# A graph layer on one Trainium2 core: three rearrangements in the second layer's small matmuls

## The chip, the cores and the metric

The kernel runs on one core of a Trainium2 chip. The metric is the device time of one execution in microseconds (us). Before the change it was 2445.93 us, the median of three runs (2436.05 to 2448.57).

## What is computed

64 graphs of 256 nodes with 256 features each go through two layers, each followed by a residual and a layer norm. Everything is fp32. The reference, cut to what matters here:

```python
# layer 0
norm_adj = d_inv_sqrt[:, :, None] * adj * d_inv_sqrt[:, None, :]
x = layernorm(x + ((norm_adj + alpha * eye) @ x) @ W.T + b)

# layer 1
xc = transpose(x)                                   # features x nodes
h = relu(bn1(conv1d(xc, conv1_w)))                  # conv1: one tap, 256 -> 256
h = bn2(conv1d(h, conv2_w))                         # conv2: 17 taps along the nodes
x_conv = transpose(relu(h + xc))
s = x @ w_se.T + b_se                               # 3 numbers per node
sq = sum(s * s, axis=-1)
dist = sq[:, :, None] + sq[:, None, :] - 2.0 * einsum('bnd,bmd->bnm', s, s)
A = exp(-dist) * adj
x_nmp = A @ relu(x @ w_msg.T + b_msg)
# a GRU cell with input [x_conv, x_nmp] and hidden state x follows, then
x = layernorm(x + gru(x_in, x))
```

## The kernel before

The 17-tap convolution is done with short Fourier transforms: the 256 nodes of a graph are cut into 16 tiles of 16 nodes, each tile is transformed with its surroundings (32 values per tile and feature), and for each frequency one product with the transformed weights is taken for 8 graphs at once. So the kernel works in rounds of 8 graphs: the graphs' first part (`layer0`, `layer1`), then the products per frequency and the transforms back on VectorE, then the GRU (`gru`), whose matmuls are mixed among those of the next round. The functions are generators; at each `yield` another one may put its instructions in, and a scheduler then fixes the order on each engine.

`layer1` of one graph, whole but for its last lines:

```python
    def layer1(g, V):
        x1, adjT = X1.pop(g), ADJT.pop(g)
        xn = work.tile([P, 2 * DCH, N], F32, name="xn")
        x1T = xn[:, :DCH]
        p = bank("p_x1T").rearrange("p (k n) -> p k n", k=DCH)
        for k in range(DCH):
            for c in range(NCH):
                nc.tensor.transpose(p[:, k, c * P : (c + 1) * P], x1[:, c, k * P : (k + 1) * P], ident)
        nc.scalar.copy(x1T, p)
        yield
        p = bank("p_s")
        for k in range(DCH):
            nc.tensor.matmul(p[:96, :N], wse[:, k, :], x1T[:, k], start=k == 0, stop=k == DCH - 1)
        nc.vector.tensor_scalar(dl[0:32, :], p[0:32, :N], bse[0:32], None, op0=ALU.add)
        nc.vector.tensor_scalar(dr[0:32, :], p[0:32, :N], bse[0:32], 2.0, op0=ALU.add, op1=ALU.mult)
        nc.scalar.activation(dr[32:64, :], p[32:64, :N], AF.Square, bias=bse[32:64])
        nc.scalar.activation(dl[64:96, :], p[64:96, :N], AF.Square, bias=bse[64:96])

        h = work.tile([P, NCH, D], F32, name="h", bufs=1)
        p = bank("p_conv1").rearrange("p (c o) -> p c o", c=NCH)
        # p[:, c, :] = x1T[:, k, chunk c].T @ wc1[:, k, :], 4 matmuls of 256 columns
        nc.vector.tensor_tensor(h, p, bn1_bias.unsqueeze(1).to_broadcast([P, NCH, D]), op=ALU.add)
        nc.scalar.activation(h, h, AF.Relu)
        yield
        # p_msg: 4 matmuls with wmsg, then the bias (VectorE) and the relu (ScalarE) into msg
        yield
        aT = work.tile([P, NCH, 2, P], F32, name="aT", bufs=1)
        p = bank("p_dist").rearrange("p (c n) -> p c n", c=NCH)
        for c in range(NCH):
            nc.tensor.matmul(p[:, c, :], dl[:, c * P : (c + 1) * P], dr, start=True, stop=True)
        nc.scalar.activation(aT.rearrange("p c n q -> p c (n q)"), p, AF.Exp)
        nc.vector.tensor_mul(aT, aT, adjT[:, :, 0:3:2, :])
        yield
        mid = GT // 2
        for k in range(DCH):
            p = bank("p_dft")
            for c, t0, t1 in ((0, 0, mid + 1), (1, mid + 1, GT), (1, mid - 1, mid + 1)):
                first = t0 + 1 - c * mid
                nc.tensor.matmul(
                    p[:, t0 * FL : t1 * FL], h[:, c, k * P : (k + 1) * P],
                    fwd[:, first : first + t1 - t0, :].rearrange("p t f -> p (t f)"),
                    start=t0 == 0, stop=t1 == mid + 1 and c == 1,
                )
            nc.scalar.copy(
                V[:, :, k, g % Q * GT : (g % Q + 1) * GT], p.rearrange("p (t f) -> p f t", f=FL)
            )
        yield
        # p_nmp: 4 matmuls of msg with aT; copied into xn and stored for the GRU
        ...
```

N = D = 256, P = 128, NCH = DCH = 2 chunks, GT = 16 tiles, FL = 32. `bank` takes one of three PSUM banks in turn. `dl` and `dr` hold three groups of 32 rows: s against 2s, -1 against s squared, s squared against -1, so that one matmul over 96 rows gives minus the distances. `layer0` of a later graph (its matmuls are p_adjT, p_hT, p_out) is mixed in between these parts, and so are the GRU's p_rz and p_n.

## Time and profile before

| | |
|---|---|
| span in the profile | 2444.4 us |
| TensorE (PE) busy | 2327.9 us, 9440 records |
| VectorE (DVE) busy | 1406.5 us, 3231 instructions |
| ScalarE (ACT) busy | 748.6 us |
| GpSimd (POOL) busy | 530.2 us |
| DMA | 289.73 MB, mean 119 GB/s |
| granted TensorE clock | 0.979 of full speed |

The groups of instructions that the change touches, as the profile gives them (records, mean duration of one):

| line, engine | what | records | mean ns |
|---|---|---|---|
| L364 PE | p_s, 256 columns | 256 | 397 |
| L374 PE | p_conv, 256 columns | 512 | 382 |
| L396 PE | p_dist, 96 rows, 256 columns | 256 | 379 |
| L407 PE | p_dft, 288 / 224 / 64 columns | 256 each | 423 / 352 / 247 |
| L358 PE | p_x1T, transposes of 128 columns | 256 | 278 |
| L365, L366 DVE | s and 2s out of PSUM, 32x256 | 64 each | 469, 463 |
| L377 DVE | bias of conv1, 128x512 | 64 | 684 |
| L367, L368 ACT | squares out of PSUM, 32x256 | 64 each | 467, 465 |
| L397 ACT | exp out of PSUM, 128x512 | 64 | 595 |

In the profile the rows of an engine are groups of equal instructions with their source line, output and inputs. PE is TensorE's matmuls, PEld its weight loads. A matmul's recorded duration contains the time in the pipeline, and records overlap: what a matmul takes from the engine is seen in the distance between the starts of neighbours. "A waited for B" in the list of waits means that A's engine sat idle until B ended. The windows view gives, for a stretch of the span, the busy time and the number of instructions of PE, PEld, DVE, ACT and POOL, then the clock, the busy share of the DMA engines and their GB/s.

### The profile page before, as it was taken

How to read it: one execution, taken by the hardware profiler on the slowest of the kernel's cores; microseconds unless marked ns; L12 is line 12 of the kernel's file. 1: busy time of each engine (PE TensorE's matmuls, PEld its weight loads, DVE VectorE, ACT ScalarE, POOL GpSimd, SP SyncE). 2: the span in 40 equal slices, each digit the busy share in tenths (PEclk: the TensorE clock that was granted, in tenths of full speed). 3: DMA queues.
4: the chain of work that ended last, by engine and by line, in shares of the span. 5: the costliest groups of instructions: out<-in, count | busy, mean ns of one | idle time of the engine just before them, and what ended most of it. 6: DMA issues, size and time to landing. Idle time of an engine off the chain costs nothing.

```text
span 2444.4 us, 27289 instructions
## 1 busy us (share of the span) xinstructions
PE 2327.9 (95%) x9440; PEld 1714.9 (70%) x9440; DVE 1406.5 (58%) x3231; ACT 748.6 (31%) x1417; POOL 530.2 (22%) x581
## 2 busy tenths in 40 slices
PE   5999799999999999999999999999999999999997
PEld 4887577766777677776877667776677767776654
DVE  4344754576546755468445674457654674446744
ACT  2563153204441144311532124420444114431111
POOL 3221122112221122221221222211222112211122
PEclk8999999999999999999999999999999999999999
DMA  6557522462225522273223722246312552126221
GB/s 152 163 170 254 148 83 77 143 172 95 65 82 178 145 91 85 88 196 111 90 78 126 206 74 91 72 149 172 95 65 82 182 141 91 65 76 185 79 74 47
DMA packets 225890, 289.73 MB, mean 119 GB/s; under 512 B 19081, under 2 KB 202633, under 8 KB 224250
## 3 DMA queue, kind: packets, MB, share of 16 engines
q1 hardware_dynamic: 188986, 207.19, 27.8%
q0 software_dynamic: 33360, 79.88, 11.6%
q8 instruction: 75, 1.23, 0.2%
q10 hardware_dynamic: 3408, 0.93, 0.2%
q14 instruction: 61, 0.50, 0.1%
HBM read 208.46 MB, written 79.47 MB: 118 GB/s over the span
## 4 chain that ended last, share of the span: by engine, by line
PE 47%; issue 32%; POOL 8%; DVE 7%; DMA 3%; ACT 2%; POOLq 0%; ACTq 0%; SPq 0%; DVEq 0%
PE p_rz L633 8%; PE p_n L638 5%; PE p_nmp L420 5%; PE p_dft L407 4%; PE p_k L444 4%; PE p_msg L385 3%; PE p_conv L374 3%; PE p_out L339 3%; PE p_hT L329 3%; PE p_u L252 2%; POOL ln_rs L269 2%; POOL total L660 2%; POOL x_g L661 2%; PE p_s L364 2%; PE p_dist L396 2%
## 5 line engine op out<-in xcount | busy, mean ns | idle before, releaser
L633 PE MATMUL p_rz<-whh,xn_g 128*128 128x512 f32 x512 | 244.9, 594 | 0.0
L633 PE MATMUL p_rz<-wih,xcT 128*128 128x512 f32 x512 | 241.2, 593 | 0.0
L633 PE MATMUL p_rz<-wih,xn_g 128*128 128x512 f32 x512 | 240.6, 592 | 0.0
L642 DVE TENSOR_TENSOR trz<-p_rz,brz_t 128x512 f32<-128x512 f32 x128 | 87.7, 685 | 242.8 <-PE p_rz L633 242.8
L660 POOL TENSOR_TENSOR total<-x_g,nn 128x512 f32<-128x512 f32 x64 | 81.5, 1273 | 657.2 <-ACT nn L652 657.0
L444 PE MATMUL p_k<-u,V 128*128 128x256 f32 x960 | 220.0, 381 | 4.0 <-DMA u<-ud 3.6
L269 POOL TENSOR_TENSOR ln_rs<-ln_rs,neg_half 128x2 f32<-128x2 f32 x128 | 99.8, 780 | 549.6 <-DVE ln_rs L268 534.5
L643 ACT ACTIVATE trz<-trz 128x512 f32<-128x512 f32 x128 | 80.7, 630 | 422.8 <-DVE trz L642 379.4
L444 PEld LDWEIGHTS p_k<-u,V 128*128 128x128 f32 x960 | 181.1, 190 | 33.8 <-DMA u<-ud 4.5
L633 PEld LDWEIGHTS p_rz<-wih,xn_g 128*128 128x128 f32 x512 | 97.3, 190 | 119.3 <-issue 119.0
L633 PEld LDWEIGHTS p_rz<-wih,xcT 128*128 128x128 f32 x512 | 96.2, 190 | 114.8 <-issue 114.7
L638 PE MATMUL p_n<-whh,xn_g 128*128 128x256 f32 x512 | 139.9, 396 | 20.4 <-DVE trz L642 20.4
L645 DVE TENSOR_TENSOR gn<-p_n,bn_t 128x512 f32<-128x512 f32 x128 | 88.2, 689 | 119.3 <-PE p_n L638 118.7
L329 PE MATMUL p_hT<-adjT,x 128*128 128x256 f32 x512 | 127.6, 397 | 25.6 <-DVE ln_rs L268 11.0
L420 PE MATMUL p_nmp<-aT,msg 128*128 128x256 f32 x512 | 132.2, 404 | 17.4 <-DVE aT L398 17.4
L407 PEld LDWEIGHTS p_dft<-fwd,h 128*128 128x128 f32 x768 | 135.1, 190 | 18.0 <-ACT xcT L598 1.0
L407 PE MATMUL p_dft<-fwd,h 128*128 128x288 f32 (+2 forms) x768 | 146.9, 341 | 0.4 <-DVE x L343 0.4
L638 PEld LDWEIGHTS p_n<-whh,xn_g 128*128 128x128 f32 x512 | 98.7, 198 | 62.6 <-issue 27.5
L638 PE MATMUL p_n<-wih,xn_g 128*128 128x256 f32 x512 | 139.6, 395 | 0.0
L638 PE MATMUL p_n<-wih,xcT 128*128 128x256 f32 x512 | 137.1, 392 | 0.0
L633 PEld LDWEIGHTS p_rz<-whh,xn_g 128*128 128x128 f32 x512 | 94.2, 190 | 58.1 <-issue 51.4
L329 PEld LDWEIGHTS p_hT<-adjT,x 128*128 128x128 f32 x512 | 102.1, 201 | 43.8 <-issue 11.8
(137 smaller groups left out, 4150.3 us busy)
## 6 DMA issues: line engine op xcount, KB each, us to landing
u<-ud SPq DMA_DIRECT2D x376, 256.0 KB
xn_d<-xn POOLq DMA_DIRECT2D x64, 512.0 KB, 2.9
xn_g<-xn_d SPq DMA_DIRECT2D x64, 512.0 KB
adj_t<-in_adj_dram SPq DMA_DIRECT2D x64, 256.0 KB
x_t<-in_x_dram SPq DMA_DIRECT2D x64, 256.0 KB
x_d<-x POOLq DMA_DIRECT2D x64, 256.0 KB, 2.6
x_g<-x_d SPq DMA_DIRECT2D x64, 256.0 KB
M<-x_d POOLq DMA_DIRECT2D x32, 512.0 KB, 11.8
```

The lines of the kernel that those rows point to most:

```text
L269: nc.gpsimd.tensor_tensor(rs, rs, neg_half[:, :NCH], op=ALU.pow)
L329: nc.tensor.matmul(p[:, k, :], x1[:, mc, k * P : (k + 1) * P], adjT[:, mc, 1 - mc : 3 - mc, :].rearrange("p n q -> p (n q)"), start=mc == ...
L339: nc.tensor.matmul(p[:, c, :], hT[:, k, c * P : (c + 1) * P], w0[:, k, :], start=k == 0, stop=k == DCH - 1)
L407: nc.tensor.matmul(p[:, t0 * FL : t1 * FL], h[:, c, k * P : (k + 1) * P], fwd[:, first : first + t1 - t0, :].rearrange("p t f -> p (t f)") ...
L420: nc.tensor.matmul(p[:, k, :], msg[:, mc, k * P : (k + 1) * P], aT[:, mc].rearrange("p n q -> p (n q)"), start=mc == 0, stop=mc == NCH - 1,)
L444: nc.tensor.matmul(p[:, j * D : (j + 1) * D], v[:, k, :], u[:, k, :], start=k == 0, stop=k == DCH - 1)
L633: nc.tensor.matmul(q, lhsT, w[:, : 2 * D], start=j == 0, stop=j == len(terms) - 1)
L638: nc.tensor.matmul(p[:, o * D : (o + 1) * D], lhsT, w[:, 2 * D :], start=j == 0, stop=j == len(terms) - 1)
L642: nc.vector.tensor_add(trz[:, c, :], q, brz_t)
L643: nc.scalar.activation(trz[:, c, :], trz[:, c, :], AF.Tanh, scale=0.5)
L645: nc.vector.tensor_add(gn, p.rearrange("p (i d) -> p i d", i=2), bn_t)
L660: nc.gpsimd.tensor_tensor(total, x1, nn, op=ALU.add)
```

## The change

Three things are rearranged, all in `layer1`.

1. *Transform.* Chunk 0 of the nodes gives tiles 0 to 8, chunk 1 gives tiles 7 to 15; tiles 7 and 8 are a sum of both. Before, chunk 1 took two matmuls: one that writes tiles 9 to 15 and one that adds to tiles 7 and 8. Now it is one matmul over tiles 7 to 15 that adds where chunk 0 has written and writes where it hasn't.
2. *s.* Before, s came from two matmuls of its own, in rows. Now its weights are three more columns of conv1's (259 instead of 256, and one bank for each chunk), so s comes out with nodes on the partitions. A few small VectorE operations build a 128-column tile with s, 2s, minus the sum of squares and ones, and two transposes turn it into rows.
3. *Distances.* The rows are now five (three of s, one each for the two sums of squares), which fit in 32. They stand twice, in rows 0 to 31 and 32 to 63, so that the two matmuls for the two chunks use different row groups of the array, with a bank each and an exp each.

Besides, the order of the parts changes (the transform now stands ahead of the distances), and `layer0` of a later graph is put in after parts 0, 1 and 5.

The diff, with the constants' set-up cut:

```diff
-    wc1 = const.tile([P, DCH, D], F32)
...
+    wc1 = const.tile([P, DCH, D + NSE], F32)
+    nc.scalar.dma_start(wc1[:, :, :D], conv1T.rearrange("(k p) o -> p k o", p=P))
+    nc.scalar.dma_start(wc1[:, :, D:], w_seT.rearrange("(k p) o -> p k o", p=P))
...
+    scols = []
+    for i in range(2):
+        t = const.tile([P, NCH, P], F32, name=f"scols{i}")
+        nc.gpsimd.memset(t, 0.0)
+        for c in (NSE, 32 + NSE, 64 + NSE + 1, 96 + NSE + 1):
+            nc.gpsimd.memset(t[:, :, c : c + 1], 1.0)
+        scols.append(t)
@@ -359,24 +359,30 @@
         nc.scalar.copy(x1T, p)
 
         yield
-        p = bank("p_s")
-        for k in range(DCH):
-            nc.tensor.matmul(p[:96, :N], wse[:, k, :], x1T[:, k], start=k == 0, stop=k == DCH - 1)
-        nc.vector.tensor_scalar(dl[0:32, :], p[0:32, :N], bse[0:32], None, op0=ALU.add)
-        nc.vector.tensor_scalar(dr[0:32, :], p[0:32, :N], bse[0:32], 2.0, op0=ALU.add, op1=ALU.mult)
-        nc.scalar.activation(dr[32:64, :], p[32:64, :N], AF.Square, bias=bse[32:64])
-        nc.scalar.activation(dl[64:96, :], p[64:96, :N], AF.Square, bias=bse[64:96])
-
         h = work.tile([P, NCH, D], F32, name="h", bufs=1)
-        p = bank("p_conv1").rearrange("p (c o) -> p c o", c=NCH)
+        s3 = small.tile([P, NCH, NSE], F32, name="s3")
         for c in range(NCH):
+            p = bank("p_conv1")[:, : D + NSE]
             for k in range(DCH):
                 nc.tensor.matmul(
-                    p[:, c, :], x1T[:, k, c * P : (c + 1) * P], wc1[:, k, :], start=k == 0, stop=k == DCH - 1
-                )
-        nc.vector.tensor_tensor(h, p, bn1_bias.unsqueeze(1).to_broadcast([P, NCH, D]), op=ALU.add)
+                    p, x1T[:, k, c * P : (c + 1) * P], wc1[:, k, :], start=k == 0, stop=k == DCH - 1
+                )
+            nc.vector.tensor_tensor(s3[:, c, :], p[:, D:], bse, op=ALU.add)
+            nc.vector.tensor_tensor(h[:, c, :], p[:, :D], bn1_bias, op=ALU.add)
         nc.scalar.activation(h, h, AF.Relu)
 
+        cols = scols[g % 2].rearrange("p c (q r) -> p c q r", r=32)
+        nsq = small.tile([P, NCH, NSE], F32, name="nsq")
+        nc.vector.scalar_tensor_tensor(nsq, s3, -1.0, s3, op0=ALU.mult, op1=ALU.mult)
+        nc.vector.tensor_reduce(cols[:, :, 0, NSE + 1 : NSE + 2], nsq, AX.X, ALU.add)
+        s3 = s3.unsqueeze(2).to_broadcast([P, NCH, 2, NSE])
+        nc.vector.tensor_copy(cols[:, :, 0:2, :NSE], s3)
+        nc.vector.tensor_scalar(cols[:, :, 2:4, :NSE], s3, 2.0, None, op0=ALU.mult)
+        sq = cols[:, :, 0:1, NSE + 1 : NSE + 2]
+        nc.vector.tensor_copy(cols[:, :, 1:2, NSE + 1 : NSE + 2], sq)
+        nc.vector.tensor_copy(
+            cols[:, :, 2:4, NSE : NSE + 1], sq.to_broadcast([P, NCH, 2, 1])
+        )
         yield
         msg = work.tile([P, NCH, D], F32, name="msg", bufs=1)
         p = bank("p_msg").rearrange("p (c d) -> p c d", c=NCH)
@@ -389,30 +395,39 @@
         nc.scalar.activation(msg, msg, AF.Relu)
         yield
 
-
-        aT = work.tile([P, NCH, 2, P], F32, name="aT", bufs=1)
-        p = bank("p_dist").rearrange("p (c n) -> p c n", c=NCH)
+        p = bank("p_rows")
         for c in range(NCH):
-            nc.tensor.matmul(p[:, c, :], dl[:, c * P : (c + 1) * P], dr, start=True, stop=True)
-        nc.scalar.activation(aT.rearrange("p c n q -> p c (n q)"), p, AF.Exp)
-        nc.vector.tensor_mul(aT, aT, adjT[:, :, 0:3:2, :])
-        yield
-
+            nc.tensor.transpose(p[:, c * P : (c + 1) * P], scols[g % 2][:, c, :], ident)
+        dl = work.tile([64, N], F32, name="dist_l", bufs=1)
+        nc.scalar.copy(dl, p[0:64, :N])
+        dr = work.tile([64, N], F32, name="dist_r", bufs=1)
+        nc.vector.tensor_copy(dr, p[64:P, :N])
+        yield
 
         mid = GT // 2
         for k in range(DCH):
             p = bank("p_dft")
-            for c, t0, t1 in ((0, 0, mid + 1), (1, mid + 1, GT), (1, mid - 1, mid + 1)):
+
+            for c, t0, t1 in ((0, 0, mid + 1), (1, mid - 1, GT)):
                 first = t0 + 1 - c * mid
                 nc.tensor.matmul(
                     p[:, t0 * FL : t1 * FL], h[:, c, k * P : (k + 1) * P],
                     fwd[:, first : first + t1 - t0, :].rearrange("p t f -> p (t f)"),
-                    start=t0 == 0, stop=t1 == mid + 1 and c == 1,
+                    start=c == 0, stop=True, skip_group_check=c == 1,
                 )
             nc.scalar.copy(
                 V[:, :, k, g % Q * GT : (g % Q + 1) * GT], p.rearrange("p (t f) -> p f t", f=FL)
             )
 
+        yield
+
+        aT = work.tile([P, NCH, 2, P], F32, name="aT", bufs=1)
+        for c in range(NCH):
+            rows = slice(32 * c, 32 * c + 32)
+            p = bank("p_dist")[:, :N]
+            nc.tensor.matmul(p, dl[rows, c * P : (c + 1) * P], dr[rows, :], start=True, stop=True)
+            nc.scalar.activation(aT[:, c].rearrange("p n q -> p (n q)"), p, AF.Exp)
+        nc.vector.tensor_mul(aT, aT, adjT[:, :, 0:3:2, :])
         yield
         p = bank("p_nmp").rearrange("p (k n) -> p k n", k=DCH)
         for k in range(DCH):
@@ -693,7 +708,10 @@
         for i in range(Q):
             load(first + i + 3)
             later = layer0(first + i + 2) if i + 2 < Q else iter(())
-            yield from merge(layer1(first + i, V), later, 1)
+            for piece, _ in enumerate(layer1(first + i, V)):
+                yield
+                if piece in (0, 1, 5) and next(later, "end") != "end":
+                    yield
             yield from later
             if between:
                 yield from between(i)
...
```

## The prediction

> **What bounds the kernel now.** I read the page's first two parts to see which engine has no idle time, then stretches of the span, then the list of what TensorE waits for, then a few microseconds of the timeline.
>
> ```profile
> PE 2327.9 (95%) x9440; PEld 1714.9 (70%) x9440; DVE 1406.5 (58%) x3231; ACT 748.6 (31%) x1417; POOL 530.2 (22%) x581
> ...
> PE   5999799999999999999999999999999999999997
> ...
> PEclk8999999999999999999999999999999999999999
> ```
>
> TensorE is busy in nearly every slice, VectorE 58%. A busy TensorE alone proves little, because its records overlap, so I asked for stretches that each hold one round of 8 graphs (busy time, with the number of instructions in brackets):
>
> ```profile
> 520.00:812.00 292.00, 283.41 (x1150) 209.28 (x1149) 172.75 (x386) 88.80 (x169) 64.48 (x69) 0.98 0.38 115
> 812.00:1102.00 290.00, 282.39 (x1149) 208.50 (x1148) 172.93 (x386) 88.79 (x169) 64.01 (x69) 0.98 0.39 115
> ```
>
> The rounds repeat to about a microsecond, TensorE (first busy column) idles 8 us in 290, VectorE (third) 117. What TensorE waits for, in total, number and longest:
>
> ```profile
> PE p_n L638 <- DVE trz L642: 20.4, 7, 3.3
> PE p_nmp L420 <- DVE aT L398: 17.4, 7, 2.6
> PE p_x1T L358 <- ACT x L279: 15.3, 13, 4.8
> PE p_hT L329 <- DVE ln_rs L268: 11.0, 1, 11.0
> ```
>
> All listed waits add up to 104 us of 2444, and 25 of those lie in the first 61 us. The page's chain gives PE 47% and "issue" 32%, which is time in which an engine waited for nothing that the profile shows; in the list of waits nearly all of it stands before TensorE's own weight loads (285 us at p_rz alone). So a graph costs what its matmuls cost in TensorE's queue, and a matmul removed there should shorten the span by its slot. The slot is the distance from start to start, not the mean duration. One pass of the timeline gives the slots:
>
> ```profile
> 1001.35 1.03 PE L396 MATMUL p_dist<-dist_r,dist_l 96*128 96x256 f32 x4
> 1002.21 2.28 PE L407 MATMUL p_dft<-fwd,h 128*128 128x288 f32 x12
> 1004.33 1.95 PE L420 MATMUL p_nmp<-aT,msg 128*128 128x256 f32 x8
> 1006.11 1.88 PE L633 MATMUL p_rz<-whh,xn_g 128*128 128x512 f32 x4
> 1007.83 1.88 PE L633 MATMUL p_rz<-wih,xn_g 128*128 128x512 f32 x4
> ```
>
> A matmul of the program leaves two records (9440 records are 4336 matmuls twice and 768 transposes once; the program has 5104). Four records of 512 columns take 1007.83 - 1006.11 = 1.72 us, so 0.43 each, 0.84 ns per column. 256 columns: 0.215 per record, 0.43 per matmul; the two distance matmuls took 0.86, as they should. Transposes of 128 columns take 0.11 each (four from 1011.26 to 1011.70).
>
> **What the Trainium skill says.** "TensorE: Matmul & The Clock Gate", section "LDWEIGHTS (loading the stationary operand)", makes a load last columns / 1.2 ns whatever the rows, 107 ns at 128 columns. The trace agrees in effect: the six transform matmuls, twelve records, take 1004.33 - 1002.21 = 2.12 us; at 0.84 ns per column the 288s take 0.24 and the 224s 0.19, which leaves (1.06 - 0.48 - 0.38) / 2 = 0.10 us for a record of 64 columns whose streaming is worth 0.054. It runs at the pace of its load. "PSUM — Partial Sum Buffer", section "The four PSUM rules": a matmul without the first flag adds where a column has been written since the last clear and overwrites elsewhere. That is what lets one matmul add to 64 columns and write 224; no row of the trace before shows it. "TensorEngine Tiling (Array Packing)", section "Key Properties": matmuls in different row tiles run in parallel, but changing the mode drains the array. Its "Gotcha 1: PSUM Pressure" adds that row tiles need different banks, which is why the distances get two. No run here shows either yet; all of before's matmuls have more than 64 rows.
>
> **The change part by part**, TensorE's queue first, per graph.
>
> Removed: the two matmuls for s (906.60 to 907.47 in the timeline), **-0.86**. Its wait for the transposed input (4.1 us in all) passes to conv1, no gain.
>
> Transform: six matmuls become four, the columns stay 1152. Twelve records of 2.12 us become eight of 0.241, 1.93: **-0.19**.
>
> Conv1: 259 columns for 256 in eight records, 24 columns x 0.84 ns: **+0.02**.
>
> Two transposes of the small columns, 0.11 each: **+0.22**.
>
> Distances: the records are low and high pass of c=0, then of c=1, in order. If the two row groups overlap, c=1's first pass can run beside c=0's second: three slots of 0.215 for four, -0.21. Entering and leaving 32-row mode drains the array twice; a drain also ends the hiding of loads (0.19 us busy each), which could eat the 0.21 and another 0.2. I take **0**, with -0.2 to +0.2.
>
> Sum -0.81 per graph. Times 64 is 52 us; graph 0 lies in the start-up, which waits for VectorE, ScalarE and DMA, so I count 63 graphs: **51 us**.
>
> VectorE: out go two 32x256 reads of PSUM (0.469 + 0.463) and one 128x512 add (0.684), 1.62 us. In come two 128x256 adds from PSUM (about 0.44, between 0.41 of L487's short form and 0.48 of L343), two 128x3 adds and six other tiny operations (0.17 each, as the 128x2 ones of L268) and a 64x256 copy (about 0.43): 2.7 us. That is +1.1 x 64 = 70 us, to some 1475 us or 62%. All of it fits in VectorE's 117 idle us per round (8 x 1.1 = 9). ScalarE: two squares (0.467 + 0.465) and an exp of 0.595 out, a 64x256 copy and two 128x256 exps in, about 0.4 each (L485's short form 0.37, L652 0.42): -0.3 per graph. Neither sets the end.
>
> **New waits.** The build shows TensorE's order. Between the last conv1 matmul and the transposes stand in 63 of 64 graphs at least 3.4 us of matmuls. The small chain needs about 0.2 (semaphore and PSUM) + 0.17 + 0.44 + 6 x 0.17 = 1.8 us, hidden by 1.6; the degree reduction, which the build puts between two of these operations and which waited 41 us on its DMA, lengthens it by 0.7 or more and is likely hidden still. Between transposes and distances stand the transforms, 1.9 us, against 0.7 for the two copies. Between distances and p_nmp stand now 1.7 us (p_out) where the transforms gave 2.1. The chain there, from the end of the distances at D: the second V copy runs from D - 0.6 to D, the exps to D + 0.75, the product (0.13 + 0.66) to D + 1.55, p_nmp at D + 1.6. It just fits. p_out itself needs the bank (three rotate) that this V copy leaves, at about D + 0.1. In 48 graphs p_out comes first after the distances: x 0.1 = +5 us. The 17.4 us of p_nmp's waits come at 2.5 us once a round; the build now puts p_real and the first p_k there, 2.2 us, and I expect half back, -8. Together **-3**.
>
> 2446 - 51 - 3 = **2392**.
>
> **Rivals.**
> (1) *The small chain takes over*: the transposes wait for VectorE, because the two adds and eight tiny operations stand in its queue behind long gate operations or behind the degree's DMA. For it: VectorE works in order, and its gate operations last 0.42 to 0.69. Against it: 3.4 us of cover. One microsecond in each of 64 graphs would bring 2392 to 2456, no gain.
> (2) *The row groups cost instead of sparing*: two drains with exposed loads, +0.4 per graph, +26 us: 2418, within 2%.
> (3) *The row groups overlap fully* and the waits stay small: -0.2 to -0.4 per graph, 2366 to 2379. But p_out's bank is then not free when the distances end, so in those 48 graphs part of it becomes a wait.
> (4) *Product before p_nmp too late*: 0.5 us in 42 graphs, +21: 2413. Speaks for it: the 0.1 us of margin.
>
> **Range and chances.** The removed slots (52 us) rest on measured distances and are firm to some 5 us. The distances give +-13, the waits -8 to +25. So 2366 to 2414. The 2% line is 2397, 5 us above my number; with a spread of about 18 us that is some 60% for faster by over 2%, nearly all the rest within.
>
> **What would show it.** TensorE's records fall from 9440 to 9056 (4080 x 2 + 896), p_s is gone, and the eight p_dft records start 0.24 apart. From p_dist's first start to the next instruction: 0.65 if the groups overlap, 0.86 if they take turns, above 1 if the drain costs. VectorE about 1475 us. A round lasts 8 x 0.8 = 6.5 us less, 284. A row "p_rows waited for DVE scols" over 15 us would prove rival 1, "p_nmp waited for DVE aT" above 25 us rival 4, "p_out waited for ACT V" the bank. I am wrong if TensorE's slots shrink as said and its idle time grows by as much.

## The result and the profile after

The change made the kernel faster, by half of what was predicted: 2419.5 us (median of four, 2413.94 to 2421.03) against 2447.25 us for the kernel before on the same chip. The ratio is 0.989, with a 95% interval of 0.9854 to 0.9926: some 27 us or 1.1%, where the prediction had 2392 us, 2.2% less, and a range that ended at 2414.

The page of the kernel after, the same lines as were shown of before (busy time of each engine, then TensorE and its granted clock in 40 slices):

```profile
PE 2272.3 (94%) x9056; PEld 1615.0 (67%) x9056; DVE 1439.1 (59%) x3740; ACT 711.3 (29%) x1417; POOL 531.0 (22%) x587
...
PE   5998799998999999999999989999899999999997
...
PEclk8999899999999999999999999999999999999999
```

TensorE has lost exactly the 384 records that the change removes, and its busy time fell by 56 us; the span fell by only 26. The difference is in the second row: four slices have turned from 9 to 8. One round of the kernel after in the windows view (length, then busy time and instructions of PE, PEld, DVE, ACT and POOL):

```profile
836.65:1125.55 288.90, 275.43 (x1100) 195.98 (x1100) 176.63 (x451) 84.41 (x170) 64.06 (x68) 0.99 0.38 116
```

The kernel before had 283.41 busy of 292 in such a stretch, 8.6 us idle; here it is 13.5. What TensorE waits for (in total, number of times, longest), from its list of waits:

```profile
PE p_x1T L358 <- ACT x L279: 25.0, 11, 6.5
PE p_n L653 <- DVE trz L657: 20.4, 7, 3.3
PE p_conv L367 <- ACT xn L359: 13.7, 23, 0.9
PE p_nmp L435 <- DVE aT L430: 12.9, 7, 1.8
PE p_hT L329 <- DVE adjT L312: 12.2, 10, 6.2
...
PE p_out L339 <- ACT V L418: 4.0, 7, 0.6
...
PE p_dist L428 <- ACT V L418: 3.5, 7, 0.7
...
PE p_rows L400 <- DVE scols L383: 1.7, 7, 0.3
```

Against before, p_x1T waits 9.7 us more, the first matmul behind the transposed input 9.6 more (4.1 at p_s before), the two V rows are new (7.5), adjT has 2.9 more, and only p_nmp has less (17.4 before). No single row explains the loss, and the row that the prediction had named for the small chain, p_rows, has 1.7 us.

To keep the accounts straight I split TensorE's time, from first record to last, in three: **idle** is the sum of the gaps in which no TensorE record runs; **half clock** is half of the active time under clock records below full speed; **work** is the rest. The three add up to the span less some 19 us at its ends.

| us | work | idle | half clock | span |
|---|---|---|---|---|
| before | 2289.0 | 98.2 | 38.5 | 2444.4 |
| after | 2240.6 | 127.6 | 31.2 | 2418.7 |
| difference | -48.4 | +29.4 | -7.3 | -25.7 |

So the work went as predicted (-51), and the idle time took most of it back. The experiments ask whose idle time this is.

### The profile page after: what moved, and what is told of

Same layout as the page of the kernel before. It is cut to its first block, busy times and chain, and to the rows that moved or that the text cites. A ratio compares the mean times of both kernels' runs of the same rounds, so it can differ in the third digit from the quotient of the medians.

```text
span 2418.7 us, 26972 instructions
## 1 busy us (share of the span) xinstructions
PE 2272.3 (94%) x9056; PEld 1615.0 (67%) x9056; DVE 1439.1 (59%) x3740; ACT 711.3 (29%) x1417; POOL 531.0 (22%) x587
## 4 chain that ended last, share of the span: by engine, by line
PE 39%; issue 32%; DVE 12%; POOL 10%; ACT 4%; DMA 2%; POOLq 0%; DVEq 0%; ACTq 0%; SPq 0%
PE p_k L459 7%; PE p_rz L648 7%; PE p_n L653 4%; PE p_conv L367 3%; PE p_out L339 3%; PE p_msg L391 3%; PE p_dft L413 3%; PE p_nmp L435 3%; POOL ln_rs L269 2%; POOL total L675 2%; POOL x_g L676 2%; PE p_u L252 2%; PE p_hT L329 2%; DVE ln_st L266 2%; POOL M L569 1%
## 5 line engine op out<-in xcount | busy, mean ns | idle before, releaser
L367 PE MATMUL p_conv<-wc,xn 128*128 128x259 f32 x512 | 134.1, 406 | 13.7 <-ACT xn L359 13.7
L413 PE MATMUL p_dft<-fwd,h 128*128 128x288 f32 x512 | 134.9, 406 | 0.0
L435 PE MATMUL p_nmp<-aT,msg 128*128 128x256 f32 x512 | 122.0, 381 | 12.9 <-DVE aT L430 12.9
```

The source lines that it names most:

```text
L367: nc.tensor.matmul(p, x1T[:, k, c * P : (c + 1) * P], wc1[:, k, :], start=k == 0, stop=k == DCH - 1)
L413: nc.tensor.matmul(p[:, t0 * FL : t1 * FL], h[:, c, k * P : (k + 1) * P], fwd[:, first : first + t1 - t0, :].rearrange("p t f -> p (t f)") ...
L435: nc.tensor.matmul(p[:, k, :], msg[:, mc, k * P : (k + 1) * P], aT[:, mc].rearrange("p n q -> p (n q)"), start=mc == 0, stop=mc == NCH - 1,)
```

## The experiments

Every ratio below is to the kernel before, run on the same chip; the bracket is its 95% interval. The changed kernel's own ratio, 0.989, is known to 9 us either way, so differences of a few microseconds to it are not clear of noise. "Work" and "idle" come from one trace of each kernel.

### The parts one at a time

**The transform alone** (on the kernel before):

```diff
-            for c, t0, t1 in ((0, 0, mid + 1), (1, mid + 1, GT), (1, mid - 1, mid + 1)):
+            for c, t0, t1 in ((0, 0, mid + 1), (1, mid - 1, GT)):
```

> The kernel before with the one-matmul transform alone. In the trace of before a graph's twelve transform records take 2.119 us, in the trace after eight take 1.942 where no change of tiling follows: 0.177 x 64 = 11 us. Theory W (the slots shrank as predicted, the loss is new waits that come with the other parts) and theory S (the loss lies in slots that are larger than booked: first weight load of conv1, drains around the distances) both expect 2436 us, ratio 0.9955. A third theory, that a round has fixed chains on VectorE and GpSimd which swallow any saving on TensorE, expects less than half of it: 2441 or more.

Measured 2436.74 us, ratio 0.9976 [0.9967, 0.9986]: about 6 us. The time lies where two of the theories had it, but the ratio doesn't: the gain is half of the 11 us that they expected.

**The new order of the parts as well**, with s and the distances still as before (the transform ahead of the distances, `layer0` put in after parts 0, 1 and 5):

```diff
-            yield from merge(layer1(first + i, V), later, 1)
+            for piece, _ in enumerate(layer1(first + i, V)):
+                yield
+                if piece in (0, 1, 5) and next(later, "end") != "end":
+                    yield
```

> The kernel before with the one-matmul transform, the new order of the parts (transform ahead of the distances) and the new placing of layer0, but s, its squares and the 96-row distances as before. Against e1_transform_only it is the order alone. Theory W with the order as cause: the waits of p_nmp, p_out and conv1 appear here too, 10 to 20 us over e1: 2446 to 2456. Theory S, or waits that come from the new small chain and its banks: as e1, 2434 to 2440.

Measured 2427.02 us, ratio 0.9936 [0.992, 0.9952]: another 10 us, where one theory expected a loss and the other no difference. Two of the longer waits are there already, before s or the distances are touched. The one for xn comes with the order (4.1 with the transform alone); the one of p_x1T had grown from 15.3 to 20.7 with the transform and grows again here:

```profile
PE p_x1T L358 <- ACT x L279: 25.5, 9, 5.1
...
PE p_s L364 <- ACT xn L359: 13.6, 23, 0.9
```

**The new s too, without the row groups** (the changed kernel, both distance matmuls in rows 0 to 31):

```diff
-            rows = slice(32 * c, 32 * c + 32)
+            rows = slice(0, 32)
```

> The changed kernel, but both distance matmuls take rows 0 to 31, one row group; two banks and two exps as after. The overlapped pair takes 0.63 us in the trace after. Theory S: four records one after the other, 0.22 to 0.30 each, 0.9 to 1.2 us, so +0.3 to +0.55 per graph, 2438 to 2455. Theory W: in the 48 graphs with p_out behind the distances the overlap is partly waiting time for the bank, so only +0.1 to +0.3 per graph, 2426 to 2438.

Measured 2425.78 us, ratio 0.9933 [0.9919, 0.9947]. Against the run before it, work fell by 13.7 us (2274.6 to 2260.9) and the time by 1: idle took 6.0 and half clock 3.6 of it. The step that brings the new s saves TensorE work and gains nothing. The time lies at the lower end of what was expected for waits (2426 to 2438). The row groups, the difference to the whole change, are worth 6 us by the medians and 10 by the ratios, which is not clear of noise.

Step by step the idle time was 98.2 us before, 102.2 with the transform, 108.2 with the order, 114.2 with the new s and 127.6 with the row groups. So 13.4 of the 29.4 new microseconds came with the last step, which takes some 20 us of work away; TensorE's order is the same in these two kernels, and the small chain is in both. Shorter TensorE work by itself lets waits out that were covered.

This is the row of the distances in the timelines of this kernel and of the changed one (start, duration, engine, line, operation):

```profile
1162.14 1.12 PE L428 MATMUL p_dist<-dist_r,dist_l 32*128 32x256 f32 x4
1163.19 0.48 PE L339 MATMUL p_out<-w,hT 128*128 128x256 f32 x1
```

```profile
1160.04 0.70 PE L428 MATMUL p_dist<-dist_r,dist_l 32*128 32x256 f32 x4
1160.14 0.59 ACT L418 COPY V<-p_dft 128x512 f32<-128x512 f32 x1 [0.33 <-PE p_dft L413]
...
1160.78 0.30 PEld L339 LDWEIGHTS p_out<-w,hT 128*128 128x128 f32 x2 [0.45 <-ACT V L418]
```

In one row group the two matmuls take 1.05 us to the next start; in two, the array is through after 0.63 (measured in the 16 graphs where something else than p_out follows), and p_out starts at 0.74 only because ScalarE's copy of V, which holds its bank, runs until 1160.73.

**The old way of putting in `layer0`** (after every part) with the changed kernel:

```diff
-            for piece, _ in enumerate(layer1(first + i, V)):
-                yield
-                if piece in (0, 1, 5) and next(later, "end") != "end":
-                    yield
+            yield from merge(layer1(first + i, V), later, 1)
```

> The changed kernel, but layer0 of the later graph is put in again after every part (parts 0, 1 and 2) as before, so that p_out stands ahead of the transposes and no longer between the distances and p_nmp. Theory W with the new placing as cause: p_out's and the distances' waits for the V copy (7.5 us) go and those of p_nmp grow, because in most graphs only a p_rz piece of 1.7 us or less stands there; 2415 to 2425. Theory S: no slot changes, 2419. If the placing itself is what costs, 2405 or less.

Measured 2473.68 us, ratio 1.0142 [1.0121, 1.0163], slower than the kernel before and than any of the theories had it. Its list of waits begins with

```profile
PE p_nmp L435 <- DVE aT L430: 37.6, 25, 2.9
```

so the product that feeds p_nmp needs the `layer0` matmuls behind the distances as cover. The new order is no ornament.

### Guesses at the new waits

**Half clock at the start of a round.** Six small matmuls ahead of a round's first p_x1T, to keep TensorE from idling there:

```diff
+        if g % Q == 0 and g >= Q:
+            p = accbank("p_warm")
+            for _ in range(6):
+                nc.tensor.matmul(p[:, :D], ident, mv[:, 0, 0:1].to_broadcast([P, D]), start=True, stop=True)
```

> The changed kernel with six added matmuls of 256 columns (2.6 us, result unused, their moving operand is a column of the layer norm's statistics so that they can't run earlier) just ahead of the first graph's p_x1T in rounds 2 to 8. There TensorE waits 2.6 or 4.1 us per round for a chain on VectorE, GpSimd and ScalarE that takes 23.2 us in all four kernels, and the records show half clock for 3.4 us or more after it. Theory C (part of the removed work comes back as half clock, because TensorE idles longer before p_x1T than the 1.2 to 1.5 us of most rounds before): the added work costs nothing, the half clock goes, 1.7 us per round, 2405 to 2411. Rival (the half clock costs nothing or moves elsewhere): 2418 to 2422. If the stretch were bound by TensorE after all: 2435.

Measured 2456.52 us, ratio 1.0049 [1.0037, 1.0062]. A miss: the scheduler put these matmuls ahead of the gates', where their input came late.

```profile
PE p_warm L364 <- DVE ln_mv L271: 43.2, 6, 7.6
```

It says nothing on the clock.

**One bank more for the small matmuls** (four and four for three and five):

```diff
-    ps = ctx.enter_context(tc.tile_pool(name="ps", bufs=3, space=bass.MemoryType.PSUM))
-    psacc = ctx.enter_context(tc.tile_pool(name="psacc", bufs=5, space=bass.MemoryType.PSUM))
+    ps = ctx.enter_context(tc.tile_pool(name="ps", bufs=4, space=bass.MemoryType.PSUM))
+    psacc = ctx.enter_context(tc.tile_pool(name="psacc", bufs=4, space=bass.MemoryType.PSUM))
```

> The changed kernel with four banks in the rotation of layer0 and layer1 and four instead of five for the products and the gates. Theory B (the new waits of p_out and the distances for the V copy, 7.5 us in all, are waits for a bank): both rows vanish from TensorE's waits and 5 to 10 us go, 2410 to 2415, if the products and gates don't need the fifth bank. Rival: they do, p_k, p_rz and p_n wait for VectorE, 2422 to 2440.

Measured 2462.22 us, ratio 1.0072 [1.0058, 1.0085], slower than either theory had it: the gates wait when they have four banks.

```profile
PE p_rz L648 <- DVE trz L657: 50.8, 6, 8.5
```

**Half of the copy of V on VectorE**:

```diff
-            nc.scalar.copy(
+            copy = nc.scalar.copy if k == 0 else nc.vector.tensor_copy
+            copy(
```

> The changed kernel with the second half of the copy of V (the one of the second 32-row distance bank) on VectorE instead of ScalarE. Theory A, the outer products and the second distance pair wait for ScalarE's copy of V because that copy stands behind the gate's and layer norm's operations: the 7.5 us of waits for ACT V fall to under 3 us, and 3 to 8 us of the time go, 2412 to 2417 us. Theory B, those waits are slack moved from elsewhere: the VectorE chain of some 0.3 us a graph more (63 x 0.3 = 19 us of VectorE work) lengthens the waits for aT and adjT by as much, and the time is 2419 to 2427 us.

Measured 2416.93 us, ratio 0.9887 [0.9867, 0.9908], which can't be told from the change itself (0.989). The wait for V changed hands and stayed:

```profile
PE p_out L339 <- DVE V L419: 4.4, 26, 0.2
```

**The start of a round filled with real work.** `layer0` of the next round's first two graphs runs between the last three product steps, and not after them:

```diff
+        head = merge(layer0(first), layer0(first + 1), 1) if more else iter(())
         sums(V, 0)
         for step in range(STEPS):
             products(V, M, step)
+            if step >= 5:
+                next(head, None)
+                next(head, None)
+        run(head)
         odd_frequencies(M)
         run(late)
-        if more:
-            run(merge(layer0(first), layer0(first + 1), 1))
```

On the changed kernel:

> The changed kernel, but layer0 of the next round's first two graphs is put among the last three steps of the products, ahead of the odd frequencies on VectorE, instead of behind them. Theory F (each round has a fixed stretch of 23.2 us bound by VectorE and GpSimd, in which TensorE idles 3.3 us before and 2.6 to 4.1 us within, and which the change can't shorten): both waits and the half clock after them go, 6 to 9 us in seven rounds, 2355 to 2378. Rival (the chain only moves into the products and stops TensorE there): 2410 or more.

Measured 2391.1 us, ratio 0.9781 [0.9767, 0.9794], between the two theories, with the work unchanged (2240.4), 19.3 us less idle and 11.3 less half clock. On the kernel before:

> The kernel before, with one move alone: the layer-0 steps of the next round's first two graphs run between the last three product steps instead of after the last odd frequencies. The same move on the changed kernel brought it from a ratio of 0.989 to 0.978, about 26 us. Theory A, the stretch between two rounds is a fixed serial chain that both kernels pay alike: then this gains here about what it gained there, 20 to 30 us, so 2417 to 2427 us, ratio 0.988 to 0.992, and the change's own worth is still some 25 us on top of it. Theory B, the idle at the start of a round is the changed kernel's own new wait (its part order leaves TensorE with less to do there): then the move gains here only 5 to 12 us, 2435 to 2442 us, and the changed kernel with the move stands about 45 us under this one, close to the 48 us of work taken away.

Measured 2413.19 us, ratio 0.9871 [0.9852, 0.989]. The edit gives this kernel 32 us and the changed one 28. It is a good edit, but the idle time it takes away is not the change's own: with it the change is worth 22 us, no more than without.

**Layer 0's layer norm off ScalarE** (its scaling stood in ScalarE's queue ahead of conv1's copy):

```diff
-        layernorm(x1, nc.scalar)
+        layernorm(x1, nc.vector)
```

On the changed kernel:

> The changed kernel with the scaling of layer 0's layer norm on VectorE instead of ScalarE. Theory A, conv1's waits for xn (13.7 us in 23 waits) and those of p_x1T for x (25 us in 11) are ScalarE's queue of layer norms ahead of the copy: the first falls to under 5 us, the second by 5 us or more, and the time is 2400 to 2412 us. Theory B, the chain at the start of a round is VectorE's and gets longer by the scaling (two of about 0.4 us each): p_x1T's wait stays at 25 us or grows with VectorE named, and the time is 2418 to 2430 us.

Measured 2391.41 us, ratio 0.9789 [0.9765, 0.9813], more than either theory gave it, and conv1's wait went as it should, while p_x1T's stayed and named VectorE:

```profile
PE p_x1T L358 <- DVE x L272: 22.5, 7, 6.2
...
PE p_conv L367 <- ACT xn L359: 3.4, 9, 0.7
```

That looked like the cause. The same edit on the kernel before decides it:

> The kernel before with the scaling of layer 0's layer norm on VectorE instead of ScalarE, the same edit that brought the changed kernel from a ratio of 0.989 to 0.979 and its waits of conv1 for xn from 13.7 to 3.4 us. Theory A, the changed kernel's new part order set conv1's copy behind these scalings in ScalarE's queue, and the kernel before never paid for that (its waits of p_s for xn are 4.1 us in all): then the edit gains here at most 8 us, 2437 to 2447 us, and the change made on top of this edit is worth 45 to 55 us, close to the 48 us of TensorE work that it takes away. Theory B, the scaling on ScalarE costs both kernels alike: then it gains here some 25 us, about 2420 us, and the change is worth about 28 us with and without it.

Measured 2417.57 us, ratio 0.9902 [0.9881, 0.9924]. It gave 23 us there too, by other waits (p_nmp's for aT fell from 17.4 to 2.9), so the theory of ScalarE's queue falls: with the edit the change is still worth only 26 us. Three more runs put the edits together. The kernel before with both:

> The kernel before with both edits, the early layer 0 of the next round (which alone gave it 2413 us) and the layer norm's scaling on VectorE. The base line for the next run. Theory A of the ScalarE queue: nothing beyond the early layer 0, 2405 to 2415 us. Theory B: 2388 to 2398 us.

Measured 2426.76 us, ratio 0.9931 [0.9904, 0.9958]: worse than with the early `layer0` alone, not clearly worse than with the layer norm's edit alone, and outside both ranges. I didn't follow it further. The changed kernel with both:

> The changed kernel with both edits. Each alone gave about 28 us (2391 us). If the waits they take away are different ones (the idle at the start of a round, and conv1's wait for xn inside it), they add: 2365 to 2378 us, and the distance to the kernel before with both edits is 35 to 48 us. If both take away the same waits, it stays at 2383 to 2392 us and the distance is under 28 us.

Measured 2387.94 us, ratio 0.9779 [0.9755, 0.9802]: the gains don't add. But in the kernel before, both together give less than either alone, so on top of both the change is worth 37 us by the ratios, give or take 9, against 22 and 26 us on top of one. What it is worth depends on how the rest is arranged. And with half of V's copy on VectorE besides:

> As the run before, with the second half of the copy of V on VectorE too. Alone it took 2.5 us and left the outer products waiting for VectorE's copy (4.4 us in 26 waits). With the scalings on VectorE as well, VectorE has some 45 us more to do in all: 2 us better to 6 us worse than the run before, most likely 0 to 4 us worse.

Measured 2391.18 us, ratio 0.9788 [0.9764, 0.9812]: no difference.

### The small chain

What was left was rival 1, whose own row (p_rows waiting for scols) had seemed to rule it out. These three runs leave out work, so what they compute is not the reference's: the attention's weights come from constants. TensorE's matmuls are all kept.

The changed kernel without the small VectorE operations that build the columns of s:

```diff
-            nc.vector.tensor_tensor(s3[:, c, :], p[:, D:], bse, op=ALU.add)
             nc.vector.tensor_tensor(h[:, c, :], p[:, :D], bn1_bias, op=ALU.add)
...
-        nc.vector.scalar_tensor_tensor(nsq, s3, -1.0, s3, op0=ALU.mult, op1=ALU.mult)
-        nc.vector.tensor_reduce(cols[:, :, 0, NSE + 1 : NSE + 2], nsq, AX.X, ALU.add)
...                                     # and the four small copies into cols
```

> The changed kernel without the small VectorE and ScalarE-free chain that makes the columns of s: the two adds of the bias, the square, the row sum and the four small copies are left out, and scols keeps the constants set once (the attention it computes is not the reference's). conv1 keeps its 259 columns, the transposes, both copies of rows and the distances stay, so TensorE's work is unchanged at about 2240 us. It leaves out some 1.3 us of VectorE a graph, 83 us in all. Theory V (rival 1 of the prediction, in a hidden form: this chain delays VectorE's other results, aT and adjT and x, and so makes the new idle time): TensorE's idle falls from 128 to under 108 us and the time to 2395 to 2404 us. Theory W (the new idle comes from the order of the parts and from shorter TensorE work between the same releases): idle stays over 116 us, the time at 2410 to 2420 us.

Measured 2402.48 us, ratio 0.9831 [0.9809, 0.9853], 17 us under the changed kernel by the medians, 14 by the ratios. The time is what theory V expected; the idle time, 110.2 us, lies between the two theories. The scheduler orders each edited program anew, and 52 of TensorE's 9056 records stand elsewhere. VectorE's busy time fell by 42.8 us (1439.1 to 1396.3), 0.67 a graph and not the expected 1.3.

Without the two copies of the rows either, so that nothing lies between conv1 and the distances but TensorE's own work:

```diff
-        dl = work.tile([64, N], F32, name="dist_l", bufs=1)
-        nc.scalar.copy(dl, p[0:64, :N])
-        dr = work.tile([64, N], F32, name="dist_r", bufs=1)
-        nc.vector.tensor_copy(dr, p[64:P, :N])
```

> As the run before, and the two copies of the transposed rows are left out too: the distances multiply constant rows, and nothing lies between conv1 and the distances but TensorE's own work. This is the counterpart of the next run. Theory V: another 0.43 us of VectorE and 0.36 us of ScalarE a graph gone, 2380 to 2398 us, TensorE idle under 100 us. Theory W: 2408 to 2418 us, idle over 112 us.

Measured 2396.71 us, ratio 0.981 [0.9788, 0.9831]. Again theory V's time, with more idle time left (106.7 us) than it said; 67 records stand elsewhere than in the changed kernel. Its counterpart is the kernel before without its four operations between the s matmul and the distances:

```diff
-        nc.vector.tensor_scalar(dl[0:32, :], p[0:32, :N], bse[0:32], None, op0=ALU.add)
-        nc.vector.tensor_scalar(dr[0:32, :], p[0:32, :N], bse[0:32], 2.0, op0=ALU.add, op1=ALU.mult)
-        nc.scalar.activation(dr[32:64, :], p[32:64, :N], AF.Square, bias=bse[32:64])
-        nc.scalar.activation(dl[64:96, :], p[64:96, :N], AF.Square, bias=bse[64:96])
```

> The kernel before without the four operations (two of VectorE, two of ScalarE) between the s matmul and the distances, with constant rows; its TensorE work is unchanged at about 2289 us. It leaves out about 0.8 us of VectorE and 0.7 us of ScalarE a graph. Theory V says that the chain of before was no cost, 2438 to 2448 us, so the change between the two kernels without their chains is worth 42 us or more, near the 48 us of TensorE work. Theory W says the change is worth about 28 us here too: both without chains lie 22 to 34 us apart.

Measured 2446.62 us, ratio 1.0006 [0.999, 1.0021]. The chain of before, 52 us of VectorE and 62 of ScalarE, cost nothing that can be measured; the chain of after, with its two copies, cost 20 to 23 us (by the ratios or the medians), uncertain by some 10. Without their chains the two kernels lie 49.9 us apart by the medians and 48 by the ratios, give or take 6, and with them 27, give or take 9. The first is the 48 us of TensorE work. The five steady rounds (from one round's long wait of p_n to that of five rounds later) show where it lies:

| us, five rounds | length | work | idle | half clock |
|---|---|---|---|---|
| before | 1452.2 | 1392.0 | 38.9 | 21.2 |
| after | 1440.7 | 1361.7 | 62.8 | 16.2 |
| before, without its chain | 1457.9 | 1391.6 | 47.0 | 19.2 |
| after, small operations left out | 1431.5 | 1361.3 | 54.1 | 16.2 |
| after, copies left out too | 1425.2 | 1363.0 | 46.7 | 15.6 |

Between the two kernels without chains, the idle time is equal and a round is 6.5 us shorter, as the prediction had worked out from the slots alone. Against the kernel before itself the round is 5.4 us shorter: leaving its chain out made that kernel's rounds 1.1 us longer in this trace, by 8.1 us more idle time in the five, with no change in the median time. Of the 15.5 us that the five rounds of the changed kernel lose, 9.2 went with the small operations and 6.3 with the copies. The lists of waits of these two, first after and then before:

```profile
PE p_x1T L360 <- ACT x L281: 18.4, 13, 5.6
PE p_conv L368 <- ACT xn L361: 13.4, 23, 0.9
...
PE p_hT L331 <- DVE adjT L314: 9.0, 4, 6.9
...
PE p_out L341 <- ACT V L402: 1.2, 6, 0.2
```

```profile
PE p_x1T L354 <- ACT x L275: 22.4, 11, 5.2
...
PE p_hT L325 <- DVE adjT L308: 9.0, 2, 8.3
...
PE p_out L335 <- ACT hT L330: 6.8, 11, 0.7
PE p_s L360 <- ACT xn L355: 4.1, 9, 0.7
```

With the chain and its copies gone p_x1T waits 6.6 us less than in the changed kernel, adjT 3.2 less, and of the 7.5 us for V 1.2 are left. The waits for V went with the copies: without the small operations alone they are still 7.8. p_x1T is a poor witness, since leaving the chain out of the kernel before raised its wait from 15.3 to 22.4. Conv1's wait stays at 13.4: that one is the order's, as the second experiment showed, which on the whole gained 10 us.

**How the chain costs what it costs** is less clear than that it does. The obvious account is that its operations push other results back in VectorE's queue. Once a round the two operations that make adjT take 3.0 us together, and p_hT needs them. The changed kernel:

```profile
1205.24 0.16 DVE L370 TENSOR_TENSOR s<-p_conv,bse 128x3 f32<-128x3 f32 x1 [1.28 <-PE p_conv L367]
...
1205.90 2.99 DVE L312 SCALAR_TENSOR_TENSOR adjT<-ident,adeg,adjT 128x128 f32<-128x128 f32 x2 [0.49 <-ACT adjT L310]
1205.92 1.88 PE L648 MATMUL p_rz<-wih,xcT 128*128 128x512 f32 x4
...
1209.04 1.53 PE L329 MATMUL p_hT<-adjT,x 128*128 128x256 f32 x6 [0.66 <-DVE adjT L312]
```

The same place without the small operations:

```profile
1189.68 3.00 DVE L310 SCALAR_TENSOR_TENSOR adjT<-ident,adeg,adjT 128x128 f32<-128x128 f32 x2 [0.23 <-ACT adjT L308]
1189.70 1.02 PE L632 MATMUL p_rz<-wih,xn_g 128*128 128x512 f32 x2
...
1190.56 1.88 PE L632 MATMUL p_rz<-wih,xcT 128*128 128x512 f32 x4
...
1192.27 2.09 PE L327 MATMUL p_hT<-adjT,x 128*128 128x256 f32 x8
```

The wait is gone, but adjT takes as long, and in the changed kernel it had not waited for the chain: ahead of it stands one operation of 0.16 us, and VectorE then sat idle for 0.49 us until ScalarE's copy was there. What differs is TensorE's order. Four records of the gates stand between conv1 and p_hT in the changed kernel, six here, and eight with the copies left out too, so TensorE has work for nearly as long as adjT takes. It is so in all five steady rounds. The 3.3 us that this wait comes to in the five rounds went because the scheduler fixed another order.

A little later in the changed kernel the queue is shared indeed:

```profile
1210.49 0.15 DVE L376 SCALAR_TENSOR_TENSOR nsq<-s 128x6 f32<-128x6 f32 x1
1210.57 0.16 DVE L379 COPY scols<-s 128x12 f32<-128x12 f32 x1
1210.64 0.68 DVE L678 SCALAR_TENSOR_TENSOR x_g<-x_g,total 128x512 f32<-128x512 f32 x1
...
1212.54 0.30 PE L400 MATMUL p_rows<-ident,scols 128*128 128x128 f32 x1 [0.25 <-DVE scols L383]
```

VectorE works without a gap from 1205.90 on, and the operations of the chain shown start 0.07 to 0.08 us apart, so each holds the queue for about that long. But what is seen to wait here is the chain itself, behind the gates and the layer norm's statistics, and TensorE's wait for it is 0.25 us. That the rest of the chain's cost comes about through this queue is argued and not shown, because the runs that leave the chain out also change the order on TensorE.

Last, the changed kernel with the early `layer0` and half of the chain on ScalarE, nothing left out:

```diff
-        nc.vector.tensor_copy(cols[:, :, 0:2, :NSE], s3)
-        nc.vector.tensor_scalar(cols[:, :, 2:4, :NSE], s3, 2.0, None, op0=ALU.mult)
+        nc.scalar.copy(cols[:, :, 0:2, :NSE], s3)
+        nc.scalar.mul(cols[:, :, 2:4, :NSE], s3, 2.0)
...                                     # the other two copies likewise
```

> The changed kernel with the early layer 0 (2391 us), and the last four small operations of the chain (two copies of s, two of its negated square) on ScalarE instead of VectorE; nothing is left out. Leaving the whole chain out gave 17 us. If what counts is VectorE's queue, taking about 0.65 of its 1.3 us a graph away gives 4 to 9 us, 2382 to 2387 us. If the chain's own length counts, the two handovers between the engines and ScalarE's queue make the transposed rows later: the wait of p_rows for scols grows from 17 us to over 25 and the time is 2391 to 2405 us.

Measured 2391.61 us, ratio 0.9786 [0.9773, 0.98], the same as with the early `layer0` alone. VectorE's busy time went down from 1421 us there to 1406, the 1406 of before, and the time didn't follow:

```profile
PE p_rows L400 <- ACT scols L383: 17.9, 12, 2.6
```

In the steady rounds p_rows waits 15.0 us instead of 4.0, and p_nmp 11.6 instead of 15.5. So handing half of the chain to ScalarE only moved the wait. What share of the chain's cost is VectorE's occupied time, what share the length of the chain and what share the order on TensorE stays open.

### A version that beats both

The early `layer0` on the changed kernel, one edit, runs at 2391.1 us, 53 us or 2.2% under the kernel before. The run with the layer norm's scaling on VectorE besides, at 2387.94, can't be told from it.

## Why the prediction was wrong

**The work was right.** -51 us predicted, -48.4 measured. By term, from the distances between starts with the idle time taken out, over the whole kernel (half clock is counted where it falls, so the terms needn't add up to 48.4):

| us | predicted (64 graphs) | measured |
|---|---|---|
| s removed | -55 | -59.5 |
| transform | -12 | -7.9 |
| conv1 | +1 | +12.4 |
| transposes | +14 | +14.2 |
| distances | 0 | -7.5 |

s and conv1 belong together. Some 0.1 us that p_s bore in 33 graphs (its first record took 0.29 us and not 0.216) conv1 bears now in 43 of 64, with 0.32; more half clock falls on conv1 too, and without half clock its term is +6.0 and that of s -57.8. The eight records of the transform start 0.243 us apart, as predicted; what is missing there is a slot of 94 ns more ahead of the distances. And the row groups overlap, so the distances gained: rival 3's mechanism, with the wait for V's bank that the prediction attached to it.

**The step that failed is "New waits", -3 us.** It measured +22: idle +29.4, half clock -7.3. The step went through the places where the change's own results are used and held each wait against its cover. Three things in it, or left out of it, were wrong.

The wait for the transposed input (4.1 us) was booked with the slots, as passing to conv1 unchanged. It became 13.7 us, and the longer wait of p_x1T, +9.7 us, is not in the sum at all. The new order of the parts brings 13.6 of the first without the chain, and the second had grown to 25.5 with it.

The small chain's length, 1.8 us, was set against 3.4 us of cover at p_rows and called hidden. At p_rows that was right (1.7 us in all). But leaving the chain and its two copies out of the changed kernel gave 20 us, uncertain by some 10, and leaving the old chain out of the old kernel gave nothing. "All of it fits in VectorE's 117 idle us per round" was an average; in the stretch shown above VectorE has no idle time. By which path the chain costs stays open, as said above.

And the cover itself was shortened: the step of the row groups alone brought 13.4 us of idle time, with TensorE's order unchanged.

**Rival 1** as it was put on record, transposes that wait for VectorE, did not come about. In a wider form, a chain that costs in rows which don't name it, it is the best supported of the four, and the sign by which I meant to know it looked at the wrong wait.

**The other signs.** 9056 records: right. A round of 284 us: it is 288, and 285 without the chain and its copies. VectorE 1475 us: 1439, mostly because the tiny operations overlap (they start 0.07 to 0.08 us apart and last 0.15). Rival 4, p_nmp above 25 us: 12.9, no; but it is real with the old way of putting in `layer0` (37.6). Rival 2, drains that cost all: no. p_out waiting for V: 4.0 us, near the +5 foreseen. p_nmp was to give back 8 and gave 4.5.

The last sentence of the prediction, that it is wrong if the slots shrink and the idle time grows by as much, came true to 29 of 48 us.

## What to carry to other kernels

A chain of tiny operations isn't free because its own consumer has cover: here the list of waits named the chain for 1.7 us, and leaving it out with its copies gave 20. To see what a suspected chain costs, leave it out of both kernels and compare the two: here that gave back the whole TensorE saving. Then compare the order of the matmuls before calling a vanished wait cured, since a scheduler may have put other work in front of it. And try every remedy on the old kernel too: two edits that seemed to cure the new waits gave the old kernel, one at a time, about as much.

## What the runs showed of the hardware

- **Row groups.** The four records of a pair in two row groups start at 0, 7, 320 and 327 ns, and the next matmul could follow at 0.63 us, against 0.865 for four 96-row records. In one 32-row group they take 1.05 us. "TensorEngine Tiling (Array Packing)", section "Key Properties", says that a change of mode drains the array; where the distances follow the transform, its last slots are 94 ns longer (2036 for 1942 ns), which fits that.
- **Half clock.** "TensorE: Matmul & The Clock Gate", section "What's actually happening", has the clock halved after an idle window of some 3.4 us. In the steady rounds the dips last 3.4 or 6.8 us. Waits of 2.6 to 3.7 us at a round's first p_x1T were each followed or met by a dip; those of 1.2 to 1.5 us, in four of before's five rounds, were not. So waits shorter than the window can cost a dip here. The length of a wait doesn't settle it: in two of the changed kernel's five rounds p_n's wait of 3.3 us had no dip behind it.
- **VectorE beside GpSimd.** The two adjT operations at 1205.90 took 2.99 us together, where the mean of one is 350 ns in before and 475 in after; GpSimd ran two 128x512 operations from 1206.12 to 1208.75. "GPSIMD Engine Reference", section "1. Specifications", says that GpSimd shares its SBUF interfaces with VectorE and contends with operations of two SBUF inputs, which this one is. Such a pair of 3.0 us comes once a round with the new order alone, in the changed kernel, with one row group, and with the chain left out. No run here takes GpSimd's operations away, so the cause stays open.
